# A graph-network megakernel on Trainium2: the first layer's edge work one turn further ahead, eight of its items at the turn's change

## The chip, the cores and the metric

The kernel runs on one core of a Trainium2 chip. The metric is the device time of one launch in microseconds (us); the median of three runs before the change is 2971.6 us. The engines are PE (matrix products), DVE (vector work), ACT (activations and copies), POOL (here the issuer of gathers and scatters by index, and of some loads) and SP (an issuer of DMAs alone). Each engine takes its instructions from a queue in order; semaphores tie the queues together.

## The reference

A batch of 32 graphs of 512 nodes with 256 features passes four layers, all over one adjacency matrix `adj` (about 1.6% of it and the diagonal are not zero). Layers 0 and 3 have this form:

```python
pre_u = einsum('bud,dk->buk', h, W1[:d]);  pre_v = einsum('bvd,dk->bvk', h, W1[d:])
hidden = relu(pre_u[:, :, None, :] + pre_v[:, None, :, :] + b1)
S = sigmoid(einsum('buvk,ko->buvo', hidden, W2)[..., 0] + b2[0])
a = einsum('buv,bud->bvd', S * adj, h)
m = einsum('uv,bud->bvd', adj, h) * h
z = beta1 * h + beta2 * (a @ Wa + ba) + beta3 * (m @ Wm + bm)
```

Layer 1 adds `relu((adj @ z) @ W.T + b)` to z. Layer 2 is attention with a softmax over all 512 nodes, with `adj` as its bias. `S` is needed only where `adj` is not zero: it is worked out for the edges alone.

## The kernel before

**Groups and turns.** The 32 graphs go in 8 groups of 4 (`NB`). For a group, `first` (line 806) turns each graph's features, multiplies them by W1 and writes both products of every node to a `table` in DRAM (`pre`, line 582: for each of 4 chunks of nodes matmuls L592 and L594, DVE operations L596, L599 and L600, a copy on ACT L597, and a table write on SP, L604, from one of three `puv` buffers). `edges` (line 650) works out S for the edges from the table. `middle` (line 839) does the rest of layer 0, layers 1 and 2, and, with `pre` again, the table for layer 3. A second pass of `edges` serves layer 3, and `last` (line 1094) ends it. The passes of `edges` are called edges0 and edges3 here. `middle` handles the four graphs one after another, here called batches 0 to 3. The `middle` of a group is a *turn*; 8 turns follow one another, turn 0 to turn 7, and turn 0 is short, since a part of its work is done ahead.

**An item.** A pass of `edges` has 36 items (`ITEMS`) of 128 edges. For each: `fetch` (line 682) gathers 128 table rows by index on POOL (L646) into one of five `rows` buffers, and where needed loads the other end's rows into one of three `mine` buffers (a plain 512 KB load on SP, L692, or a gather for the last four panels); DVE adds both (L731); then the relu, the product with W2 and the sum are four DVE operations (L747, even items) or one on DVE (L739) and, one item later, four sums on ACT (L717, odd items). The order of items begins with chunk 0 four times, then chunks 0 and 2 in turn. Every four items an exponential on ACT (L614) and a sigmoid on DVE (L618, L619, L675) follow some items later, and then POOL scatters the values of each item into `cells` in DRAM (`put`, L639). `own_1` does the same for the diagonal and sends it out on SP (L670). When all puts have landed, `load` (line 766) brings the cells back as SA, four loads on POOL (L772). `fetch` runs three items ahead (`LEAD`).

**The order of the work.** `sparse_path` (line 1162) gives each piece of each stream a time, in turns: `middle` of group t runs from `start` = t - 0.47 to `end` = start + 1 (turn 0 from 0 to 0.53). `weave` (line 454) sorts all pieces by time and issues them in that order, with one exception. The pieces of `first` and `last` are fillers: when their time comes they are put into a waiting list (`due`), and are taken out of it where a piece of `middle` says that PE has room (so many us, for instance 4.0 after zT, 7.0 at the first step of softmax), or when more than 12 wait, or all at once when a stream of a certain kind, such as edges0, begins:

```python
elif j == 0 and kind != "free":
    while due:
        fill()
room = run(k, j)
...
while room and room > 0.3 and due:
    room -= fill()
```

The order within an engine's queue is then settled by a scheduler at compile time that takes, of the instructions which it holds to be ready, the one that was issued first. `behind` (line 515) keeps the edge items' DVE and ACT operations from being taken forward by more than about two pieces of `middle`; fetches are not held so.

**Places.** In terms of the turn in which they run, before the change: edges3 of the group before has its items from 0.05 to 0.48 and its last puts to 0.54; `first` of the next group has its pieces from 0.18 to 0.44; edges0 of the next group has its first fetches from 0.448, its items from 0.495 to 0.94 and its last puts to 0.96; `last` of the group before runs from 0.56 to 0.16 of the turn after. A turn begins with SA's load and two matmul groups each of hWa and mhT (its product with `hT` on DVE is L801), byS (L891) and zT (L898, L896 on ACT, L899 on DVE); then come zW (L912), yT (L46, L922, L923), feats (L934), softmax (L958 to L964, and transposes L1003), the product with eT (L46, L981), `pre` for layer 3, and two transposes L992.

Of the kernel before, what the change touches and what calls it, by code (L numbers as in the profile page):

```python
# [31 lines left out]
LEAD = 3  # L32
LEAD_AT_ENDS = 5
TAIL = 6
EARLY = 20
CELLS = HALF * N
ITEMS = NC * OWN + 2 * PANELS
# [385 lines left out]
class Sparse:  # L423
# [223 lines left out]
            out=rows, out_offset=None, in_=g.table, in_offset=bass.IndirectOffsetOnAxis(ap=at, axis=0)  # L647
        )

    def edges(self, g, spare=(), own_tags=()):  # L650

# [67 lines left out]
        for n in range(lead):  # L721
            fetch(n)
            yield

        todo = [(2, lambda: self.exp_of(w, own)), (4, own_1)]
        done = 0
        for k in range(ITEMS):
            for _ in range(2 if spare and len(ready) > 2 else 1):
                put()
            rows, other = fetched.pop(k)  # L730
            self.behind(nc.vector.tensor_tensor(rows, rows, other, ALU.add))  # L731
            if k + lead < ITEMS:
                fetch(k + lead)
            if summed:
                summed.pop(0)()
# [385 lines left out]
def even(n):  # L1121
    return [1.0] * n
# [20 lines left out]
    return first + spread(even(ITEMS), a, b) + spread(even(TAIL), b, behind)  # L1143


def middle_shares(given):


    hWa = [] if given else [1.7, 1.7]
    shares = list(hWa)  # L1150
    for b in range(NB):
        more = hWa if b < NB - 1 else []
        shares += [] if given else [2.8, 2.8]
        shares += [3.4, 3.4, 1.0, 2.7]
        shares += [1.7, 3.4, 2.8, 4.5] + [0.9] * NC
        shares += [0.4, 0.4, 0.4, 1.0, 0.4, 1.0] + more + [1.5, 1.5]
        shares += [2.8, 4.5] + [0.4] * NC + [0.5, 0.5]
    return shares + [0.1]
# [3 lines left out]
def sparse_path(ctx, m, counts, xr, outr, B):  # L1162
# [10 lines left out]
    for t in range(last + 1):  # L1173
# [3 lines left out]
        if t == 0:  # L1177
            first = spread(FIRST, -0.385, -0.30)
            edges0 = edge_times(-0.292, -0.27, -0.03, -0.02, LEAD_AT_ENDS)
        elif t == 1:  # L1180
            first = spread(FIRST, -0.28, -0.06)
            edges0 = edge_times(0.02, 0.07, start - 0.06, start - 0.04)
        else:
            first = spread(FIRST, start - 0.82, start - 0.56)
            edges0 = edge_times(start - 0.552, start - 0.505, start - 0.06, start - 0.04)
        edges3 = edge_times(end + 0.003, end + 0.05, end + 0.48, end + 0.54)
        behind = end + 0.56, end + 1.16
        if t == last - 1:
            edges3 = edge_times(end + 0.003, end + 0.05, end + 0.46, end + 0.5)
            behind = end + 0.7, end + 1.06  # L1190
        if t == last:
# [2 lines left out]
            behind = end + 0.29, end + 0.45  # L1194
        streams += [
            (sp.first(g0, t * NB), first, FIRST_US),
            (sp.edges(g0, ("yT", "mhT0", "hWa0") if t == 0 else ()), edges0, ""),
            (sp.middle(g0, g3, t * NB), spread(middle_shares(t == 0), start, end), "main"),
            (
                sp.edges(g3, *((("yT", "h1", "hT1"), ("mhT0", "hWa0")) if t == last else ())),  # L1200
# [249 lines left out]
```

## Time and profile before

| what | value |
| --- | --- |
| runs of the kernel | 2968.61, 2971.6, 2972.93 us, median 2971.6 |
| profiled execution | 2998.45 us, span 2996.8 us |
| mean granted PE clock | 0.959 |
| DMA | 677.30 MB, mean 226 GB/s |
| first L891 of turns 0 to 7 | 245.2, 485.2, 824.2, 1168.8, 1514.9, 1864.3, 2207.9, 2551.5 us |

From one first L891 to the next turn 0 is 240 us long, turn 1 339, and turns 2 to 6 between 343.6 and 349.4. The page's 40 slices of the span show how evenly the engines are filled (each digit is a tenth):

```profile
## 2 busy tenths in 40 slices
PE   6367787989998999989999899989999899988998
PEld 3134344545664566546664466646565466644666
DVE  6874786889588885988778885888858896783494
ACT  3553454445344443544344443445434453453262
POOL 2662463646445673556536464466735564361183
PEclk9678998999999999999999999999999999999999
```

PE's line is near 9 from turn 1 on. DVE's line goes down every four or five slices: this is the change from one turn to the next, at which the last items of one pass of `edges` are done and the next pass still waits for its table. A busy PE is not PE at its peak, since the ends of matmuls are modelled; the starts are measured.

### The profile page before, as it was taken

Reading aid. Unit: us, or ns where it says so; the run is one execution under the profiler, and the core shown is the slowest. Engines: PE = TensorE matmul, PEld = TensorE weight load, DVE = VectorE, ACT = ScalarE, POOL = GpSimd, SP = SyncE. Lnnn points to the kernel's source line nnn. Section 1 sums busy time; section 2 is a strip of 40 time slices with the busy share of each in tenths; the row PEclk is TensorE's granted clock in tenths of the full one; section 3 lists DMA queues with packets and bytes.
Section 4 is the critical chain, followed back from the end, with each engine's and each line's share of the span. In section 5 each row is a group of like instructions: output and inputs, shape, how many; then the busy total and the mean of one; then the engine's idle time right before and its main releaser. Section 6 shows DMA issues by size and latency. Waiting matters only on the chain. (4 is left out here: it accounts for less than half of the span.)

```text
span 2996.8 us, 32453 instructions
## 1 busy us (share of the span) xinstructions
PE 2690.0 (90%) x8645; PEld 1613.9 (54%) x8646; DVE 2307.1 (77%) x6035; ACT 1336.8 (45%) x4101; POOL 1555.3 (52%) x1328
## 2 busy tenths in 40 slices
PE   6367787989998999989999899989999899988998
PEld 3134344545664566546664466646565466644666
DVE  6874786889588885988778885888858896783494
ACT  3553454445344443544344443445434453453262
POOL 2662463646445673556536464466735564361183
PEclk9678998999999999999999999999999999999999
DMA  8875657796678867787677866687677866663474
GB/s 268 286 225 169 213 174 221 233 300 203 217 217 269 268 211 227 230 262 254 209 222 247 275 207 230 216 268 253 211 228 236 303 227 197 208 211 102 148 244 150
DMA packets 302143, 677.30 MB, mean 226 GB/s; under 512 B 52608, under 2 KB 170880, under 8 KB 293760
## 3 DMA queue, kind: packets, MB, share of 16 engines
q0 software_dynamic: 122688, 414.40, 42.9%
q1 hardware_dynamic: 160304, 223.52, 23.0%
q10 hardware_dynamic: 18960, 37.24, 3.4%
q8 instruction: 70, 1.15, 0.2%
q14 instruction: 121, 0.99, 0.1%
HBM read 529.02 MB, written 146.01 MB: 225 GB/s over the span
## 5 line engine op out<-in xcount | busy, mean ns | idle before, releaser
L646 POOL DMA_INDIRECT rows<-table,iv x552 | 679.0, 1230 | 795.5 <-DMA table<-puv 262.7
L639 POOL DMA_INDIRECT cells<-s,cell x576 | 697.6, 1211 | 420.6 <-DVE s L675 243.2
L731 DVE TENSOR_TENSOR rows<-rows,mine 128x1024 f32<-128x1024 f32 x552 | 666.4, 1215 | 101.4 <-DMA rows<-table,iv 72.8
L717 ACT ACTIVATE rows<-rows 128x256 f32<-128x256 f32 x1088 | 439.6, 406 | 445.4 <-DVE rows L739 396.6
L46 PE MATMUL pst<-adj,h 128*128 128x512 f32 x1024 | 452.2, 592 | 0.0
L747 DVE SCALAR_TENSOR_TENSOR rows<-rows,L_gnn_W2bc 128x256 f32<-128x256 f32 x1120 | 414.0, 417 | 1.6
L739 DVE SCALAR_TENSOR_TENSOR rows<-rows,L_gnn_W2bc 128x1024 f32<-128x1024 f32 x272 | 329.4, 1213 | 0.4
L46 PEld LDWEIGHTS pst<-adj,h 128*128 128x128 f32 x1024 | 192.8, 190 | 219.9 <-issue 217.6
L46 PE MATMUL pst<-L_gnn_Wa,hT 128*128 128x256 f32 x1024 | 248.8, 393 | 62.9 <-DMA hT<-xT 57.8
L46 PEld LDWEIGHTS pst<-L_gnn_Wa,hT 128*128 128x128 f32 x1024 | 198.9, 199 | 103.0 <-issue 59.2
L46 PE MATMUL pst<-eT,feats 128*128 128x512 f32 x512 | 237.7, 619 | 10.9 <-ACT eT L1004 10.9
L46 PE MATMUL pst<-adjT,zW 128*128 128x512 f32 x512 | 228.2, 599 | 11.6 <-ACT zW L916 9.7
L596 DVE TENSOR_TENSOR puv<-pst,bc_L_gnn_b 128x256 f32<-128x256 f32 x256 | 104.9, 416 | 162.4 <-DMA table<-puv 89.2
L597 ACT COPY puv<-pst 128x256 f32<-128x256 f32 x256 | 93.2, 371 | 288.1 <-DVE puv L596 225.9
L1061 PE MATMUL pst<-hWa,SA 128*128 128x256 f32 x896 | 220.3, 400 | 0.0
L1061 PEld LDWEIGHTS pst<-hWa,SA 128*128 128x128 f32 x896 | 213.8, 328 | 3.7 <-issue 1.7
L717 ACT ACTIVATION_READ_ACCUMULATOR rows<-rows 128x1 f32 x1088 | 204.7, 188 | 0.0
L860 ACT COPY flat<-SA 128x512 f32<-128x512 f32 x128 | 136.7, 1128 | 136.6 <-issue 62.9
L891 PE MATMUL pst<-flat,hWa 128*128 128x512 f32 x448 | 196.8, 592 | 0.0
L592 PE MATMUL pst<-w_L_gnn_W,hT 128*128 128x512 f32 x256 | 141.5, 681 | 53.9 <-ACT hT L579 36.5
L46 PEld LDWEIGHTS pst<-eT,feats 128*128 128x128 f32 x512 | 99.9, 198 | 133.2 <-issue 113.3
L46 PEld LDWEIGHTS pst<-adjT,zW 128*128 128x128 f32 x512 | 96.5, 191 | 133.4 <-issue 114.0
(176 smaller groups left out, 3984.2 us busy)
## 6 DMA issues: line engine op xcount, KB each, us to landing
table<-puv SPq DMA_DIRECT2D x256, 256.0 KB
SA<-cells POOLq DMA_DIRECT2D x64, 1024.0 KB
h<-in_x_dram SPq DMA_DIRECT2D x64, 512.0 KB
mine<-table SPq DMA_DIRECT2D x64, 512.0 KB
hT<-xT SPq DMA_DIRECT2D x36, 512.0 KB
xT<-hT ACTq DMA_DIRECT2D x32, 512.0 KB
x2T<-yT SPq DMA_DIRECT2D x32, 512.0 KB
x2s<-x ACTq DMA_DIRECT2D x64, 256.0 KB
```

The costliest lines, as they stand in the source:

```text
L46: nc.tensor.matmul(out, lhsT, rhs, start=(n == 0), stop=(n == len(pairs) - 1))
L592: nc.tensor.matmul(pp, hT[:, 0, ks], w["W1"][:, 0::DC, :], start=True, stop=False)
L596: nc.vector.tensor_tensor(puv[:, 0, :], pp[:, 0:D], w["b1bc"], ALU.add)
L639: ins = self.nc.gpsimd.indirect_dma_start(out=g.cells[half], out_offset=bass.IndirectOffsetOnAxis(ap=at, axis=0), in_=s, in_offset=None)
L646: self.nc.gpsimd.indirect_dma_start(out=rows, out_offset=None, in_=g.table, in_offset=bass.IndirectOffsetOnAxis(ap=at, axis=0))
L717: self.behind(nc.scalar.activation(part, part, AF.Identity, accum_out=g.s[:, k, b : b + 1]))
L731: self.behind(nc.vector.tensor_tensor(rows, rows, other, ALU.add))
L739: nc.vector.scalar_tensor_tensor(by_entry, by_entry, 0.0, w2, ALU.max, ALU.mult)
L747: nc.vector.scalar_tensor_tensor(part, part, 0.0, w["W2bc"], ALU.max, ALU.mult, accum_out=at)
L860: self.nc.scalar.copy(flat[:, r, :], SA[r][:, :, b])
L891: nc.tensor.matmul(pz, hWa[:, r, cs], flat[:, r, :], start=(r == 0), stop=False)
L1061: self.nc.tensor.matmul(pz[:, k * D : (k + 1) * D], SA[r][:, cs, b], hWa[:, r, :], start=(r + k == 0), stop=(alone and k == 1 and r == NC ...
```

## The change

`first` of group t runs one turn earlier than before, at the same place within its turn (0.18 to 0.44); that of group 2 goes to turn 0, from 0.1 to 0.47. From group 2 on, edges0 is cut in two. Its first eight items (`SOON`) run one turn earlier, at the change into that turn: fetches from -0.017, items from 0 to 0.045. Then the pass stops, `mine` is forgotten and fetched anew, three fetches follow at 0.53, and the other 28 items run from 0.57 to 0.94, with the last puts to 0.96 as before. edges3 has its first fetch at 0.046 for 0.003, its items from 0.06 to 0.54 for 0.05 to 0.48, and its last puts to 0.57; `last` begins at 0.58 for 0.56. The last two groups' edges3 and `last`, and edges0 of groups 0 and 1, keep their times. Nothing that is computed changes.

```diff
+SOON = 8
...
-    def edges(self, g, spare=(), own_tags=()):
+    def edges(self, g, spare=(), own_tags=(), soon=0):
...
+        stop = soon or ITEMS
         todo = [(2, lambda: self.exp_of(w, own)), (4, own_1)]
         done = 0
         for k in range(ITEMS):
+            if k == stop:
+                stop = ITEMS
+                mine.clear()
+                for n in range(k, k + lead):
+                    fetch(n)
+                    yield
             for _ in range(2 if spare and len(ready) > 2 else 1):
                 put()
             rows, other = fetched.pop(k)
             self.behind(nc.vector.tensor_tensor(rows, rows, other, ALU.add))
-            if k + lead < ITEMS:
+            if k + lead < stop:
                 fetch(k + lead)
...
+def edge_times_soon(t0, t1, ahead, a, b, behind):
+
+    step = (t1 - t0) / SOON
+    first = [t0 - (LEAD - j) * step for j in range(LEAD)] + [t0 + j * step for j in range(SOON)]
+    step = (b - a) / (ITEMS - SOON)
+    first += [ahead + j * min(step, (a - ahead) / LEAD) for j in range(LEAD)]
+    return first + spread(even(ITEMS - SOON), a, b) + spread(even(TAIL), b, behind)
...
         else:
-            first = spread(FIRST, start - 0.82, start - 0.56)
-            edges0 = edge_times(start - 0.552, start - 0.505, start - 0.06, start - 0.04)
-        edges3 = edge_times(end + 0.003, end + 0.05, end + 0.48, end + 0.54)
-        behind = end + 0.56, end + 1.16
+            first = spread(FIRST, 0.1, 0.47) if t == 2 else spread(FIRST, start - 1.82, start - 1.56)
+            edges0 = edge_times_soon(
+                start - 1.0, start - 0.955, start - 0.47, start - 0.43, start - 0.06, start - 0.04
+            )
+        edges3 = edge_times(end + 0.046, end + 0.06, end + 0.54, end + 0.57)
+        behind = end + 0.58, end + 1.16
...
-            (sp.edges(g0, ("yT", "mhT0", "hWa0") if t == 0 else ()), edges0, ""),
+            (sp.edges(g0, ("yT", "mhT0", "hWa0") if t == 0 else (), soon=SOON if t > 1 else 0), edges0, ""),
```

## The prediction

> **What bounds the kernel now.** I read the page first. Its line of busy times says that PE is the fullest engine; the rest had to say where PE is not full.
>
> ```profile
> PE 2690.0 (90%) x8645; PEld 1613.9 (54%) x8646; DVE 2307.1 (77%) x6035; ACT 1336.8 (45%) x4101; POOL 1555.3 (52%) x1328
> ```
>
> Then I cut the trace at the first L891 matmul of every batch (the timeline of L891), and took the busy time of each engine between two such starts. The rows below are, in this order: the whole of turn 0, batches 0 to 3 of turn 3, batches 0 and 1 of turn 6, batches 0, 1 and 2 of turn 7.
>
> ```profile
> core 0: us, PE busy (x) PEld busy (x) DVE busy (x) ACT busy (x) POOL busy (x), PEclk, DMA share, GB/s
> 245.20:485.20 240.00, 195.90 (x561) 103.66 (x560) 159.06 (x423) 113.08 (x291) 94.74 (x87) 0.89 0.56 183
> 1168.80:1250.10 81.30, 81.30 (x276) 50.30 (x275) 70.67 (x176) 38.62 (x120) 37.02 (x32) 1.00 0.73 228
> 1250.10:1347.10 97.00, 81.25 (x239) 41.49 (x238) 81.33 (x247) 43.00 (x130) 57.96 (x52) 0.96 0.79 255
> 1347.10:1426.00 78.90, 76.99 (x262) 48.10 (x260) 70.13 (x176) 39.78 (x124) 47.08 (x38) 1.00 0.77 259
> 1426.00:1514.90 88.90, 88.90 (x301) 57.46 (x300) 59.81 (x168) 33.60 (x93) 46.64 (x41) 1.00 0.64 209
> 2207.90:2289.20 81.30, 81.30 (x276) 50.30 (x275) 70.61 (x176) 38.59 (x120) 37.50 (x32) 1.00 0.73 227
> 2289.20:2384.40 95.20, 81.00 (x240) 41.40 (x239) 81.24 (x246) 42.85 (x129) 59.23 (x52) 0.96 0.81 263
> 2551.50:2626.80 75.30, 74.57 (x253) 46.87 (x252) 59.16 (x148) 33.94 (x99) 30.32 (x27) 1.00 0.66 213
> 2626.80:2695.60 68.80, 57.96 (x165) 31.71 (x164) 59.50 (x150) 36.00 (x113) 47.34 (x41) 0.90 0.65 203
> 2695.60:2757.60 62.00, 53.98 (x165) 29.73 (x164) 28.41 (x94) 23.04 (x45) 10.23 (x12) 0.97 0.39 132
> ```
>
> A steady turn is bound by PE: in batches 0, 2 and 3 of turn 3 it idles 0, 1.9 and 0 us, though DVE is 87 to 89% busy in the first two. All that is left to win sits in batch 1, where `first` is woven in: 97.00 - 81.25 = 15.8 us. Turn 0, which has neither `first` nor `last` as filler, idles 44 us.
>
> Next, the waits of batch 1, of PE and of DVE (time, times, longest):
>
> ```profile
> PE pst L1003 <- DVE ex L964: 6.0, 3, 3.3
> PE pst L592 <- ACT hT L579: 3.6, 1, 3.6
> PE pst L592 <- DVE both L600: 2.1, 1, 2.1
> PE pst L934 <- DVE yT L923: 1.6, 1, 1.6
> ...
> DVE puv L596 <- DMA table<-puv: 7.1, 4, 3.4
> ```
>
> Most of batch 1's idle belongs to `first` itself: its transposes wait for a copy (L579), and its `puv` buffers hold DVE until a table write has landed (7.1 us). Edge items matter for L923 and a part of L964 alone.
>
> Last, the turn's change: DVE between the last `pre` of a turn and the first item of `edges3`, and POOL over the same stretch (brackets: idle before, releaser).
>
> ```profile
> 1159.94 0.08 DVE L600 DVE_READ_ACCUMULATOR both<-both,L_gnn_W2bc 128x1 f32 x1
> 1165.56 0.69 DVE L801 TENSOR_TENSOR mhT<-pst,hT 128x512 f32<-128x512 f32 x1 [5.54 <-PE pst L46]
> 1169.00 0.69 DVE L801 TENSOR_TENSOR mhT<-pst,hT 128x512 f32<-128x512 f32 x1 [2.74 <-PE pst L46]
> 1171.24 2.53 DVE L731 TENSOR_TENSOR rows<-rows,mine 128x1024 f32<-128x1024 f32 x2 [1.56 <-issue]
> ...
> 1142.47 1.17 POOL L772 DMA_DIRECT2D SA<-cells  x2 [1.66 <-issue]
> 1164.94 1.00 POOL L646 DMA_INDIRECT rows<-table,iv  x1 [21.30 <-DMA table<-puv]
> ```
>
> DVE has 5.5 + 2.7 + 1.6 us free here and POOL 21.3 us. The eight items are put into this hole.
>
> **The change, part by part.** The sum is made against the profiled execution: span 2996.8 us, 2998.45 us with what lies around it. The shown runs have a median of 2971.6 us, 27 us less; I carry the same difference in us over.
>
> *Turn 6 loses `first(7)`* (each `first` moves a turn ahead, so turns 0 to 5 hold the six that turns 1 to 6 held). Turn 7 already shows what batches 0 and 1 are with `last` pieces in batch 0, no `first`, and `edges3` beside them. Batch 0: 81.3 to 75.3, 6.0 less. Batch 1: 95.2 to something between 62.0 (turn 7's batch 2, hardly an edge item) and 68.8 (its batch 1, more items than here); I take 67, near the second: 28. Together -34 (bounds -32 and -39).
>
> *Turn 0 gains `first(2)`.* PE work of one `first`: four batches of 16 128x512 matmuls and 8 transposes. In the timeline four such matmuls start 1.72 us apart from the next four (1150.73, 1152.45), and 8 transposes take 0.87 (1157.60 to 1158.47): 4 x (4 x 1.72 + 0.87) = 31.0 us. What of it fills idle time follows from the weave's rule, due times against room. Softmax, where L1003 idles 31.7 us of turn 0, has room 7.0 at its first step, but the pieces come due one by one and are taken by the rooms of zT, yT and feats before it. So they fill the small waits before L912 (2.9) and L934 (2.4) of three batches in four, 4.0 us, and two 0.9 us pieces fall into softmax: 5.8 in all. 31.0 - 5.8 = 25; DVE's 16 x 3 `pre` operations (419 ns each, 20 us) stand in queues that softmax waits in, one more us: +26. Its DMAs (512 KB loads on SP, transposes out on ACT's queue, table writes on SP) come into a stretch with a DMA share of 0.56. Bounds: +19, if the pieces cover all 12.0 us that PE waits in turn 0 elsewhere than before L1003; +36, if `first` stretches a batch here as it does in batch 1 (95.2 - 67 = 28 us for 81.0 - 58.0 = 23 us of PE work).
>
> *Thinner edge items in the old places.* `edges3` goes from 36 items in 0.43 of a turn to 36 in 0.48, the rest of `edges0` from 36 in 0.445 to 28 in 0.37. Batch 1 (0.27 to 0.55 of the turn, counted from 1158.5, where a turn's first hWa matmul stands) gets 20 items for 22: 2 x 2.45 us less DVE (one item: L731 1.2 and L739 1.2, or L731 and four L747 that start 0.35 apart). Only the waits on L923, on the `s` operations and part of L964 can shrink, 2 us of 15.8; five turns (1 to 5): -10. Bounds 0 and -25 (5 a turn, all that is not `first`'s own). Batches 0, 2 and 3 have nothing to give.
>
> *The eight items at the turn's change, turns 1 to 6.* Their fetches can be issued before and between SA's loads and their table was written a turn before, so POOL's 21.3 us hide them; SA was landed by 1149.25, when ACT began to copy it, and PE wants it at 1168.80, so three fetches of 1.25 us ahead of it cost nothing (without that slack 3.8 us). On DVE all eight stand behind L600 (1160.0), since `behind` holds them there, and in the queue ahead of the middle's work: three items and the first L801, three more with own_1's sigmoid and the second L801, then two. Six items, 1160.0 + 6 x 2.45 + 2 x 0.69 + 0.57 = 1176.7; PE needs the second L801 for its third L898 matmul, 1175.66 + 0.86 = 1176.5: 0.2 us late. Behind it come two more items, a sigmoid (0.5), and two items of `edges3`, then L899: 1176.7 + 4.9 + 0.5 + 4.9 + 1.3 = 1188.3, where PE starts L912 at 1184.28 behind 5.2 us of `last` pieces: 4.0 late; or, if L899 is queued ahead of `edges3`'s first rows, 1183.4 and not late. Bounds 0 and 4.2 a turn. I take 1, nearer to nothing, as batch 2 with DVE at 89% costs PE 1.9 us in a whole batch: six turns, +6 (0 to +25).
>
> A row speaks on what such a stall adds. After the 3.60 us wait at L592 (1265.89) four matmuls took 2.51 us and two 1.91, for 1.88 and 1.02 elsewhere: 1.5 us more; after 2.08 us (1302.50) nothing. So the upper bound becomes 6 x 5.7 = +34. The Trainium skill, TensorE: Matmul & The Clock Gate, section Why this matters for your kernels, says that gaps over some 3 us put the clock back; by it a 4 us stall pays this and my 1 us does not, as the rows have it.
>
> A rule speaks against the place as such: GPSIMD Engine Reference, section Specifications, has GpSimd share its SBUF interfaces with VectorE and contend with DVE instructions of two SBUF inputs, as the items' are. The trace agrees: a fetch took 0.94 us with DVE idle (1170.03) and 1.68 beside L739 (1175.42). Eight fetches by 0.7 are 6 us of POOL's 21.3, so the sum stays by either.
>
> *Small parts.* `mine.clear()` loads chunks 0 and 2 once more: 12 x 512 KB over the run, at 226 GB/s 28 us of a DMA share of 0.74, behind work; SP's queue takes them where it took `edges0`'s own loads. The sums of item 7 are held until item 8, half a turn on, and with them one of five `rows` buffers through the whole of `edges3`. In turn 3 each fetch would then wait for the fourth release before it; 6.3 us pass from fetch to use (1164.94 to 1171.24), and at 4.1 us an item four buffers turn in 16.4 us, with 5 us of DVE and ACT in it: 5 us spare. Behind a waiting fetch on POOL stand puts, and for these only SA's load, half a turn later. own_1's diagonal goes out on SP's queue, with `edges3`'s `mine` loads behind it, which wait for the table anyway (1164.94). +2 (0 to +12).
>
> Sum: -34 + 26 - 10 + 6 + 2 = -10. Span 2986.8, median **2962 us**; by its own bounds mostly 2948 to 2969.
>
> **The rivals.**
>
> *The stall at the change decides (slower).* The eight items and `edges3`'s first two stand ahead of L801 and L899, PE waits 4.2 us and 1.5 for the clock. For it: DVE takes its queue in order. Against: 5.2 us of `last` pieces and L891's 6.9 us lie before each of the two points. Price 5.7 x 6 = 34 in place of 6: 2990. It decides from 2.7 us a turn, where the sum is zero.
>
> *Four `rows` buffers starve `edges3` (slower).* Late rows at the head of DVE's queue, 3 to 5 us a turn in place of 0.3: 2985. Against: the 5 us spare above.
>
> *The ends cancel, and the items do not leave batch 1's waits shorter (no change).* Turn 0 pays 33 for turn 6's 34, thinning gives nothing, the stall 0, small parts 2: 2973. For it: no edge item stands between 1296 and 1318 us in DVE's queue, while L964 is late.
>
> *Batch 1 was held by edge items after all (much faster).* Half of its 15.8 goes in five turns, -40: 2932. Against: the waits above.
>
> **How the numbers follow.** Forecast 0.45, stall 0.27, no change 0.15, four buffers 0.07, much faster 0.06. 0.2% is 6 us, about what this measurement can tell from none. Faster: 0.45 + 0.06 = 0.51; same 0.15; slower 0.27 + 0.07 = 0.34. The range has thinning and turn 0 at their good ends (15 + 7 us less, 2940) and the stall at 5.7 (2990), a little more on that side: 2940 to 2992.
>
> **What would show it.** Right: turn 6 some 310 us for 343.6, turn 0 some 266 for 240, batch 0 of turns 1 to 6 within 2 us of 81.3, batch 1 near 94. Wrong: an idle PE before L898 or L912 in batch 0 of each turn (the stall); L731 waiting for `rows` in `edges3` (buffers); batch 1 at 97 (no thinning); turn 0 at 275 or more.

## The result, and the profile after

The changed kernel has a median of 3023.87 us (four runs, 3014.21 to 3028.1) beside 2970.67 us for the kernel before in the same set of runs: ratio 1.0167, interval 1.0149 to 1.0186. It is 1.7% slower, and the time lies above the predicted range.

The profiled execution of after has a span of 3021.0 us and took 3022.74, as its other runs did. The profiled execution of before took 27 us more than its other runs, so the two traces explain a difference of 24.2 us in the span and not the whole 53 us of the medians; what the remainder is no trace shows. The second profiles of both kernels (e0 and e5 below) differ by 36.2 us. The engines' busy times are as they were. The work is the same; it waits elsewhere.

```profile
PE 2686.0 (89%) x8645; PEld 1623.0 (54%) x8646; DVE 2313.8 (77%) x6035; ACT 1335.8 (44%) x4101; POOL 1559.0 (52%) x1328
```

Line numbers of after are those of before plus 1 up to `sums` (L592 is L593, L646 is L647, L717 is L718) and plus 8 from the items' additions on (L731 is L739, L739 is L747, L747 is L755, L772 is L780, L891 is L899, L923 is L931, L934 is L942). Cut at the first L899 of every batch, these are turn 0, batches 0 to 3 of turn 3, and batches 0, 1 and 2 of turn 6; the columns are start and end, length, and the busy time of each engine.

```profile
core 0: us, PE busy (x) PEld busy (x) DVE busy (x) ACT busy (x) POOL busy (x), PEclk, DMA share, GB/s
241.40:505.50 264.10, 223.73 (x657) 120.46 (x656) 182.25 (x499) 120.47 (x318) 95.32 (x90) 0.92 0.63 206
1202.60:1286.60 84.00, 81.74 (x275) 50.19 (x274) 77.90 (x197) 41.45 (x130) 42.91 (x33) 1.00 0.77 235
1286.60:1369.10 82.50, 76.81 (x240) 40.45 (x239) 72.45 (x216) 41.42 (x125) 50.55 (x43) 1.00 0.80 256
1369.10:1456.60 87.50, 76.61 (x253) 47.76 (x252) 68.76 (x183) 38.61 (x120) 50.13 (x43) 0.94 0.74 255
1456.60:1547.90 91.30, 90.57 (x309) 59.03 (x308) 62.97 (x174) 33.57 (x90) 49.06 (x43) 1.00 0.64 220
2247.90:2325.70 77.80, 75.27 (x253) 46.58 (x252) 69.76 (x174) 36.77 (x115) 40.74 (x32) 1.00 0.77 228
2325.70:2401.20 75.50, 58.35 (x165) 32.44 (x164) 65.86 (x177) 36.83 (x116) 52.69 (x47) 0.89 0.66 212
2401.20:2485.20 84.00, 76.65 (x254) 47.49 (x253) 67.82 (x180) 38.85 (x120) 47.58 (x41) 0.98 0.76 250
```

Against before: batch 1 of turn 3 fell from 97.0 to 82.5 us, but batch 0 rose from 81.3 to 84.0, batch 2 from 78.9 to 87.5, batch 3 from 88.9 to 91.3. In batch 2 PE is busy 76.6 of 87.5 us. Its waits and DVE's and POOL's there (engine, line, what for: total, times, longest), one view each:

```profile
PE pst L942 <- DVE yT L931: 9.6, 1, 9.6
```

```profile
DVE rows L739 <- DMA rows<-table,iv: 15.4, 3, 8.7
```

```profile
POOL rows L647 <- ACT rows L718: 9.5, 3, 7.2
POOL SA L780 <- DMA cells<-s,cell: 7.1, 2, 4.8
```

The chain is read in POOL's queue over the same stretch (start, length, instruction; in brackets the idle time before it and what ended it), and then in DVE's:

```profile
1377.77 0.58 POOL L780 DMA_DIRECT2D SA<-cells  x1 [4.79 <-DMA cells<-s,cell]
1378.65 1.02 POOL L647 DMA_INDIRECT rows<-table,iv  x1 [0.30 <-issue]
1379.97 1.74 POOL L640 DMA_INDIRECT cells<-s,cell  x1 [0.30 <-DVE hT L907]
...
1385.03 1.98 POOL L640 DMA_INDIRECT cells<-s,cell  x1 [0.30 <-issue]
1387.31 0.99 POOL L647 DMA_INDIRECT rows<-table,iv  x1 [0.30 <-issue]
1388.31 0.60 POOL L780 DMA_DIRECT2D SA<-cells  x1
1391.27 1.08 POOL L780 DMA_DIRECT2D SA<-cells  x2 [2.36 <-DMA cells<-s,cell]
1392.65 1.00 POOL L647 DMA_INDIRECT rows<-table,iv  x1 [0.30 <-issue]
```

```profile
1384.94 1.23 DVE L739 TENSOR_TENSOR rows<-rows,mine 128x1024 f32<-128x1024 f32 x1 [2.35 <-DMA rows<-table,iv]
1394.83 1.22 DVE L739 TENSOR_TENSOR rows<-rows,mine 128x1024 f32<-128x1024 f32 x1 [8.66 <-DMA rows<-table,iv]
...
1403.58 1.23 DVE L739 TENSOR_TENSOR rows<-rows,mine 128x1024 f32<-128x1024 f32 x1 [4.43 <-DMA rows<-table,iv]
...
1405.54 0.69 DVE L931 TENSOR_TENSOR yT<-yT,hT 128x512 f32<-128x512 f32 x1
```

`last`'s first load of SA waits 4.79 us at the head of POOL's queue, for cells that `edges3`'s puts have only just written. Behind it stand one fetch, four puts of `edges3`'s other half (e3 below shows whose they are), and then the fetch of a further row that `edges0` needs at its restart. That fetch goes out at 1387.31, and DVE's addition of its row waits 8.66 us. The fetch after it goes out at 1392.65, behind the other three loads of SA, and DVE waits another 4.43 us for its row. L931 stands in DVE's queue behind both additions, and PE waits 9.6 us for L931's yT.

### The profile page after: what moved, and what is told of

Same layout as the page of the kernel before. It is cut to its first block, busy times and chain, and to the rows that moved or that the text cites. A ratio compares the mean times of both kernels' runs of the same rounds, so it can differ in the third digit from the quotient of the medians.

```text
span 3021.0 us, 32437 instructions
## 1 busy us (share of the span) xinstructions
PE 2686.0 (89%) x8645; PEld 1623.0 (54%) x8646; DVE 2313.8 (77%) x6035; ACT 1335.8 (44%) x4101; POOL 1559.0 (52%) x1328
## 5 line engine op out<-in xcount | busy, mean ns | idle before, releaser
L647 POOL DMA_INDIRECT rows<-table,iv x552 | 678.2, 1229 | 898.4 <-ACT rows L718 246.7
L739 DVE TENSOR_TENSOR rows<-rows,mine 128x1024 f32<-128x1024 f32 x552 | 666.7, 1218 | 187.5 <-DMA rows<-table,iv 165.8
L718 ACT ACTIVATE rows<-rows 128x256 f32<-128x256 f32 x1088 | 439.7, 407 | 541.1 <-DVE rows L747 539.6
L755 DVE SCALAR_TENSOR_TENSOR rows<-rows,L_gnn_W2bc 128x256 f32<-128x256 f32 x1120 | 414.6, 418 | 1.4
L747 DVE SCALAR_TENSOR_TENSOR rows<-rows,L_gnn_W2bc 128x1024 f32<-128x1024 f32 x272 | 331.2, 1219 | 0.6
L47 PE MATMUL pst<-eT,feats 128*128 128x512 f32 x512 | 231.1, 605 | 28.0 <-ACT eT L1012 28.0
L718 ACT ACTIVATION_READ_ACCUMULATOR rows<-rows 128x1 f32 x1088 | 205.7, 189 | 0.0
L868 ACT COPY flat<-SA 128x512 f32<-128x512 f32 x128 | 137.8, 1137 | 153.4 <-PE pst L47 84.9
L942 PE MATMUL pst<-WT,yT 128*128 128x257 f32 x512 | 134.8, 419 | 71.9 <-DVE yT L931 71.9
L899 PE MATMUL pst<-flat,hWa 128*128 128x512 f32 x448 | 196.8, 592 | 0.0
```

Of the source, the lines that this page charges most:

```text
L47: nc.tensor.matmul(out, lhsT, rhs, start=(n == 0), stop=(n == len(pairs) - 1))
L647: self.nc.gpsimd.indirect_dma_start(out=rows, out_offset=None, in_=g.table, in_offset=bass.IndirectOffsetOnAxis(ap=at, axis=0))
L718: self.behind(nc.scalar.activation(part, part, AF.Identity, accum_out=g.s[:, k, b : b + 1]))
L747: nc.vector.scalar_tensor_tensor(by_entry, by_entry, 0.0, w2, ALU.max, ALU.mult)
L755: nc.vector.scalar_tensor_tensor(part, part, 0.0, w["W2bc"], ALU.max, ALU.mult, accum_out=at)
L868: self.nc.scalar.copy(flat[:, r, :], SA[r][:, :, b])
```

## The experiments

The kernel before had medians between 2971 and 2997 us in the sets of runs, so kernels are compared by their ratio to the before of their own set. The traces are cut as above: turns 0, 1 and 6 whole, and the mean of turns 2 to 5 for batches 0 to 3, in us.

| kernel | ratio (95%) | turn 0 | turn 1 | batches 0, 1, 2, 3 | turn 6 |
| --- | --- | --- | --- | --- | --- |
| before, first profile | 1 | 240.0 | 339.1 | 81.3, 95.0, 80.0, 89.5 | 343.6 |
| before, second (e0) | 1 | 239.3 | 340.3 | 81.3, 93.4, 81.0, 90.0 | 343.4 |
| after, first | 1.0167 (1.0149 to 1.0186) | 264.2 | 349.4 | 84.4, 85.4, 87.2, 91.3 | 326.8 |
| after, second (e5) | 1.0143 (1.0127 to 1.0160) | 262.2 | 354.8 | 85.0, 85.3, 87.4, 91.3 | 331.6 |
| e1 first alone | 1.0047 (1.0021 to 1.0073) | 261.8 | 337.7 | 81.3, 93.9, 82.0, 89.7 | 329.9 |
| e2 sums at once | 1.0014 (0.9994 to 1.0033) | 261.7 | 341.1 | 83.0, 85.4, 85.5, 91.3 | 326.2 |
| e3 puts at the change | 1.0082 (1.0055 to 1.0108) | 263.8 | 351.3 | 84.5, 85.8, 84.7, 91.5 | 325.1 |
| e6 e2, last later | 1.0359 (1.0338 to 1.0380) | 264.2 | 357.0 | 87.8, 87.2, 85.8, 99.9 | 326.5 |
| e8 e2, fetches sooner | 1.0065 (1.0046 to 1.0085) | 264.3 | 345.3 | 83.5, 84.8, 84.6, 91.3 | 322.7 |
| e9 e2, load behind fetches | 0.9998 (0.9976 to 1.0019) | 263.1 | 341.3 | 83.3, 84.9, 82.9, 91.3 | 323.3 |
| e11 e2, group 2 whole | 1.0018 (0.9997 to 1.0039) | 254.9 | 346.3 | 84.5, 85.2, 83.7, 92.0 | 323.6 |
| e14 e2, edges3 sooner | 0.9992 (0.9974 to 1.0011) | 263.0 | 343.9 | 85.7, 87.6, 77.5, 91.3 | 319.1 |
| e16 e14, sums held | 1.0212 (1.0193 to 1.0232) | 263.2 | 349.5 | 87.9, 95.5, 76.5, 91.3 | 324.7 |
| e17 e14, four items | 0.9978 (0.9958 to 0.9998) | 260.3 | 328.8 | 83.3, 89.0, 76.9, 90.6 | 323.1 |
| e10 before, mine on POOL | 1.0043 (1.0017 to 1.0069) | 233.6 | 344.0 | 81.3, 95.8, 79.0, 92.0 | 348.3 |
| e15 before, edges0 later | 1.0068 (1.0043 to 1.0092) | 239.1 | 338.5 | 81.3, 93.5, 77.7, 93.5 | 345.5 |
| e18 before, copy on DVE | 1.0122 (1.0088 to 1.0155) | 239.2 | 340.2 | 82.5, 97.4, 81.1, 90.0 | 352.8 |
| e20 before, e14's places | 1.0037 (1.0019 to 1.0056) | 239.2 | 333.0 | 82.1, 89.8, 82.0, 94.6 | 345.5 |

**The kernel before once more (e0), and first alone (e1).** e1 is the kernel before with the one line

```diff
-            first = spread(FIRST, start - 0.82, start - 0.56)
+            first = spread(FIRST, 0.1, 0.47) if t == 2 else spread(FIRST, start - 1.82, start - 1.56)
```

> The kernel before, unchanged, for a second profiled execution: the first (span 2996.8 us) took 27 us more than the median of the plain runs. If profiled executions as such run longer, this one has a span near 2997 too and turns 1 to 6 of 339 to 349 us again. If the first was an odd one, the span is near 2970, and some 27 us are missing from the turns: the turns' lengths of after have then to be read against these shorter ones, and turn 6 of after lost less than it seems, or the steady turns got longer than they seem.

> Half of the change alone: first one turn further ahead, edges0 and edges3 as before. Theory (the split of edges0 costs the time: late rows hold DVE and yT in batch 2 and in batch 0 of turns 1 to 6): batch 2 of a steady turn is back at 78 to 80 us, batch 1 stays near 95, turn 0 is near 264, turn 6 near 310, and the time is 2960 to 2972, the kernel before or a little less. Rival (first one turn ahead costs it, by its table writes and loads in another place): batch 2 stays at 86 to 88 and the time is above 3000.

e0's span is 2999.4 us and its turns 2 to 5 are as long as the first's (345.7 and 345.8 us in the mean), so before's first trace was no odd one. Whether profiled executions run longer as such stays open: e0's 3001.12 us lie within the other runs of its set (2981.26 to 3005.71 us, median 2991.22). e1 took 0.5% more than before, between the totals of the two theories (before's time or less; some 1% more). Batch 2 was near the theory's (82.0, with 80.0 and 81.0 in the two traces of before), so it is the split that makes batch 2 long. Batch 1 stayed at 93.9: `first` of another group does not shorten it. But the ends do not cancel. Turn 0 pays 22.5 us and turn 6 gets back 13.5. Turn 0, and batches 0 and 1 of turn 6 of e1:

```profile
244.20:506.00 261.80, 223.57 (x657) 119.71 (x656) 176.86 (x487) 120.57 (x314) 91.99 (x86) 0.91 0.61 196
2231.00:2308.30 77.30, 74.79 (x254) 46.76 (x252) 67.60 (x165) 37.41 (x116) 39.72 (x33) 1.00 0.70 218
2308.30:2393.10 84.80, 58.11 (x165) 31.93 (x164) 66.80 (x192) 35.34 (x109) 58.08 (x50) 0.84 0.72 233
```

Without `first`, PE has 58.1 us to do in batch 1, but DVE still has the edge items, and PE idles 26.7 of the 84.8 us, 20.1 of them for DVE.

**Item 7's sums at once (e2), the puts at the change (e3), after again (e5).** e2 and e3 are the changed kernel with one of these edits:

```diff
-                if spare:
+                if spare or k + 1 == stop:
                     summed.pop(0)()
```

```diff
                 todo.pop(0)[1]()
+            if k + 1 == stop:
+                while ready:
+                    put()
             yield
```

> The changed kernel, but the four sums of item 7 are issued at once, so that no rows buffer is held from the turn's change to the restart of edges0. Theory one (POOL's queue at the restart: a load of SA for last waits there for the cells, and four puts stand before the late fetches): batch 2 keeps its 86 to 88 us, and batch 0 too, time within 8 us of 3023. Theory two (one of five rows buffers held starves edges3 and the restart): the waits of POOL for rows fall from 247 and 241 us to near the 103 and 106 of before, batch 0 goes back to 81, batch 2 gains as well, time 2990 or less.

> The changed kernel, but the four puts of items 0 to 3 are issued at the turn's change, not one each at the restart. Theory one in its one form (the puts, some 1.7 us of POOL each, delay the fetch of item 11): the waits of L739 for rows at the restart (8.7 us) fall by about 6 us, the wait of PE for yT in batch 2 (10 to 12 us a turn) by half or more, time 2985 to 3000. In its other form (the load of SA that waits 4.8 us for the cells at the head of POOL's queue): batch 2 gains 2 us or less a turn, time 3010 to 3023. Theory two (a held rows buffer): no change, 3020 or more.

> The changed kernel itself, run again beside its variants, since the runs of before on another chip had a median 20 us above the first ones. If the cost of the change does not hang on the chip, the ratio is again near 1.017; then issuing the sums of item 7 at once (1.0014) was worth 1.5%, and issuing the four puts at the turn's change (1.0082) 0.8%. If it is near 1.008, the first measurement was an unlucky pair and the puts were worth nothing.

After held its ratio (1.0143). One line for the held sums takes nine tenths of the loss away (1.0014 for 1.0143), most of it in turn 1 (13.7 us against e5) and batches 0 and 2 (2 us each in turns 2 to 5). The two ratios come from different sets; in e5's own set the kernel nearest to e2 is e8 below, at 1.0065, so the line is worth 0.8 to 1.3%. Theory two's time for it came nearly (2997.4 us for 2990 or less), its sign did not: the waits of POOL for rows, 247 and 241 us in after, are 261 and 231 in e2. What did change is the time from a row's fetch to its use, worked out from the starts of L647 and L739, in turns 2 to 5:

```
                 batch 0: median   batch 1: median, below 8 us
before           14.0 us           13.1 us          12 of 75
after             9.2 us            9.1 us          29 of 71
e2                10.5 us           12.0 us          10 of 72
```

With four buffers rows come late more often: in batch 1, 29 rows had less than 8 us, and 10 in e2. In batch 0 most of the fall from 14.0 us is still there in e2, so that part is not the held buffer's. DVE's waits for rows fell from 172.0 us (64 times) in e5 to 147.3 (44) in e2; before has 72.8 and 81.2. e3's puts brought less (1.0082). Its trace shows why it could not do what was expected of it: four puts still stand between SA's load and the next fetch in batch 2 of turn 3, though those of items 0 to 3 had gone out at the change. They are `edges3`'s.

**Which of load and fetch comes first (e6, e7, e8, e9).** All contain e2. e6: `last` from 0.66 of a turn in place of 0.58. e7: e6 with e3's edit. e8: the restart's fetches from 0.49 in place of 0.53. e9: the load gets an order behind the last fetch issued before it:

```diff
+        self.fetched = ins.ins.name
...
+            if layer == 3:
+                order = mybir.DependencyInfo(mybir.DependencyClass.NoSync, mybir.DependencyReason.DATA)
+                self.tc.add_manual_dep(ins.ins, self.fetched, order, reason="behind the fetches before")
```

> Item 7's sums at once, and last begins 0.08 of a turn later, so that its loads of SA no longer stand in POOL's queue ahead of the restart's fetches. Theory one (the load that waits for cells at the head of POOL's queue makes the rows late): the wait of 6 to 9 us of DVE for rows at the restart goes, batch 2 falls from 85 to 86 us to 80 or less, time 15 to 30 us under the version with the sums at once alone, ratio 0.991 to 0.997. Rival (the four puts between are what delays, or the items themselves): batch 2 gains 2 us or less, ratio 1.000 to 1.002.

> As the version with item 7's sums at once and last later, and with the four puts of items 0 to 3 issued at the turn's change too. If the puts at the restart matter beside the load, batch 2 gains 2 to 5 us more than without, ratio 0.988 to 0.995; if they do not, it is within 0.2% of the version without; if they take POOL's time where SA's loads for the turn itself stand, batch 0 gets longer by 1 to 2 us and the ratio is higher.

> Item 7's sums at once, and the restart's three fetches 0.04 of a turn earlier, ahead of edges3's last puts and of the load of SA instead of behind them; last at its place. Theory one: the rows of items 8 to 10 are there in time, but the fetch of item 11 still stands behind the waiting load and the puts, so batch 2 gains about half of what the later load gives, ratio 0.995 to 1.000. Rival (five rows buffers do not suffice for both passes): POOL waits there for a buffer, SA's load and edges3's last puts get later, batch 2 stays at 85 us, ratio 1.000 or more.

> Item 7's sums at once, and the loads of SA for last may not be queued on POOL ahead of a row fetch that was issued before them; everything else in its place. (In the version with last 0.08 later the load stood in POOL's queue where it was before, behind the same fetch, so that run didn't move it; it moved last's matmuls out of batch 2.) The load now stands two fetches later. Theory one (the load at the head of POOL's queue makes the rows late): DVE's wait for rows at the restart falls from 9 us to 4 or less, batch 2 from 85 to 86 us to 80 to 82, ratio 0.990 to 0.998. Rival (edges3's end itself, so late that no order helps): batch 2 within 2 us, ratio 1.000 to 1.005.

e6 was a miss that teaches: 3.6% slower than before. The scheduler took the load forward to the very place where it had been, and only `last`'s matmuls moved. Batches 2 and 3 of turn 4 of e6:

```profile
1755.80:1844.90 89.10, 72.39 (x214) 42.26 (x213) 68.71 (x184) 37.10 (x111) 46.67 (x42) 0.90 0.72 232
1844.90:1945.00 100.10, 98.16 (x341) 65.86 (x340) 63.45 (x173) 33.54 (x91) 49.18 (x43) 1.00 0.64 211
```

Batch 2 has 214 matmuls in place of 253 and is no shorter; the 31 that batch 3 got beyond its 310 make it 9 us longer. Here a filler that missed the idle time it was to fill cost its full length. e7 was no better (ratio 1.0387). e8 left batch 2 within 1 us of e2's, as the rival had it. In e9 two fetches of batch 2 stand ahead of the first load where e2 has one, and batch 2 gained 2.6 us, with a ratio of 0.9998. That lies between the theory's (80 to 82 us) and the rival's: the order counts for a part. All four loads still stand ahead of the next fetch, and the puts are as late as in e2.

**edges3 sooner (e14), with the sums held (e16), with four items (e17).** e14 is e2 with the places below; e16 is e14 without e2's edit; e17 is e14 with `SOON = 4`.

```diff
-                start - 1.0, start - 0.955, start - 0.47, start - 0.43, start - 0.06, start - 0.04
+                start - 1.0, start - 0.955, start - 0.51, start - 0.47, start - 0.06, start - 0.04
-        edges3 = edge_times(end + 0.046, end + 0.06, end + 0.54, end + 0.57)
+        edges3 = edge_times(end + 0.046, end + 0.06, end + 0.5, end + 0.53)
```

> Item 7's sums at once, edges3's items end at 0.50 and its puts at 0.53 of a turn (in place of 0.54 and 0.57) and edges0 starts again at 0.49 and 0.53 (in place of 0.53 and 0.57), so that the cells have landed when the load of SA comes, with a fetch between load and load as before the change. Theory one: batch 2 falls from 85 to 86 us to 79 to 81 as before the change, batch 1 stays near 85, ratio 0.985 to 0.993. Rival (the thinner edges3 was what made batch 1 short): batch 1 goes to 90 or more and takes back what batch 2 gains, ratio 0.999 to 1.004.

> As the version with edges3 and the restart sooner, but with item 7's sums held until the restart as in the changed kernel. It prices the held rows buffer where nothing waits for cells. Theory (four buffers in place of five shorten the time from fetch to use in edges3 from 12 to 20 us to 6 to 10 and DVE's queue then stands before late rows): batches 0 and 2 1.5 to 3 us longer a turn, turn 1 10 us, ratio 1.006 to 1.013. Rival (it only hurt together with the waiting load): ratio 0.998 to 1.002.

> As the version with edges3 and the restart sooner (item 7's sums at once), but with four items at the turn's change in place of eight, the other 32 from 0.53 to 0.94. If the eight items' DVE work is what makes batch 0 longer (81.3 to 85.7 us, and 73.5 to 86.6 in turn 1), both fall by about half of that, 2 us a turn and 6 in turn 1; batch 1 or 2 gets some of it back; ratio 0.994 to 0.999. If what stands at the change costs it whatever the number (the loads of mine, own_1's diagonal), batch 0 stays within 1 us of 85.7 and the ratio at 0.999 to 1.002.

In e14 batch 2 came back to 77.5 us, and the waits of SA's loads for cells fell from 64.8 us (16 times) in e2 to 21.9 (7 times). So its length came with these places. e14 moves `edges3`'s end and the restart at once; e8 had moved the restart's fetches alone and gained 1 us, so the late end of `edges3` is the likely part, which no run moved alone. The theory's ratio did not come; the rival's did (0.9992), but not by its way alone: batch 1 rose to 87.6 and batch 0 to 85.7. e16 prices the held buffer where few loads wait for cells (22.8 us, 7 times). The waits of DVE for rows in e14:

```profile
DVE rows L739 <- DMA rows<-table,iv: 55.6, 36, 6.9
```

and in e16:

```profile
DVE rows L739 <- DMA rows<-table,iv: 106.9, 60, 12.5
```

Twice the waits, and turns 2 to 5 are 351.2 us for 342.1: here one buffer of five is 9 us a turn, and 2.2% in the ratio (between two sets). The median time from fetch to use falls from 11.3 to 9.1 us in batch 0 and from 11.9 to 9.9 in batch 1. Batch 1 takes most of it (87.6 to 95.5 us), where the expectation had batches 0 and 2. With the change's own places the same buffer cost 3.8 us a turn and 13.7 in turn 1 (e5 against e2): what it costs hangs on the places. e17 is the price of the eight items themselves. Batches 0 of turns 1 and 4 of e17:

```profile
501.20:574.30 73.10, 61.91 (x187) 34.25 (x186) 65.80 (x169) 37.82 (x118) 40.96 (x32) 0.91 0.76 233
1508.00:1591.30 83.30, 83.30 (x284) 51.85 (x283) 70.81 (x177) 38.90 (x120) 39.54 (x32) 1.00 0.71 234
```

With four items PE does not idle in batch 0 (83.30 of 83.30 us, with 284 matmuls for the 276 of before), and turn 1's batch is as before (73.1). With eight it was 85.7 and 86.6. So a good half of what batch 0 lost was the number of items. e17 is 0.2% faster than the kernel before, and the only version here whose interval lies below 1, if barely.

**What a first costs where PE idles (e11).** e2, but group 2 is not split, has before's places, and its `first` runs from 0.15 to 0.78, into turn 1's first batch, which has no filler (turn 1's `edges3` and `last` have before's places too):

```diff
+            first = spread(FIRST, 0.15, 0.78) if t == 2 else spread(FIRST, start - 1.82, start - 1.56)
```

> Item 7's sums at once, and group 2's edges are not split and stand where they stood before the change, so its first has time to 0.78 (from 0.15) and reaches into the first batch of turn 1, where PE has no filler and idles 15 us. If the price of the ends is what their places make it: turn 0 falls from 262 to some 250, turn 1 stays at 335 to 341, time 6 to 15 us under the version with the sums at once alone, ratio 0.996 to 0.999. Rival (a first costs its 23 us wherever it goes, since pieces fill no idle time there either): the sum of turns 0 and 1 stays at 603 us, ratio 1.000 to 1.003.

The rival's: turn 0 gave 6.8 us back and turn 1 paid 5.2, turns 0 and 1 are 601.2 us for 602.8 and were 579 before. The turns pay some 22 us in either place, though PE idles 44 us in turn 0 of before.

**Why batch 1 became shorter (e10, e15, e18, e19, e20).** All but e19 are edits of the kernel before. e10: the `mine` loads issued by POOL. e15: `edges0` later. e18: first's copy on DVE. e19: that in e17. e20: e15 with `edges3` in e14's place.

```diff
-                    nc.sync.dma_start(t, places[c, 0])
+                    nc.gpsimd.dma_start(t, places[c, 0])
```

```diff
-            nc.scalar.copy(hT[:, c, :], pt)
+            nc.vector.tensor_copy(hT[:, c, :], pt)
```

```diff
-            edges0 = edge_times(start - 0.552, start - 0.505, start - 0.06, start - 0.04)
-        edges3 = edge_times(end + 0.003, end + 0.05, end + 0.48, end + 0.54)
+            edges0 = edge_times(start - 0.51, start - 0.47, start - 0.06, start - 0.04)
+        edges3 = edge_times(end + 0.046, end + 0.06, end + 0.5, end + 0.53)
```

> The kernel before, with the plain loads of mine issued by POOL instead of SP. It tests why the change made batch 1 some 10 us shorter although DVE has as many items there: in the trace of before a mine load waits 5.5 us at the head of SP's queue in batch 1, with first's table writes behind it, for which DVE then waits (8.7 us at L596). Theory (SP's queue): batch 1 falls from 94 to 86 to 90 us, DVE's wait for table writes there to 5 us or less, ratio 0.985 to 0.993. Rival (batch 1 gained by other means, such as the order of DVE's queue): batch 1 stays at 92 to 95, ratio 0.999 to 1.004, above 1 if POOL's fetches then wait behind the loads.

> The kernel before, with the whole of edges0 0.035 to 0.04 of a turn later (fetches from 0.49, items from 0.53 to 0.94 in place of 0.448 and 0.495), nothing else. It tests what made batch 1 some 8 to 10 us shorter after the change. Theory (two or three items that leave the end of batch 1, where two passes of edges overlap): batch 1 falls from 94 to 86 to 89 us without any split and without a first moved, batch 2 rises by 1 to 3, ratio 0.988 to 0.996. Rival (it is the eight items that run elsewhere, or the first that belongs to a later group): batch 1 stays at 92 or more, ratio 0.998 to 1.004.

> The kernel before, with first's copy of its turned features (two 128x512 copies a graph) on DVE in place of ACT. In batch 1 of before that copy stands in ACT's queue behind four sums of an odd edge item, which wait 3.0 to 3.1 us each for the item's DVE operation, and PE waits 3.6 us for the copy. Theory (batch 1's length is set by where the odd items' sums stand relative to that copy, and the split only shifted them): PE's idle before first's first matmuls falls from 7 to 9 us to 2 to 4, batch 1 from 93.4 to 87 to 90 without any split, ratio 0.991 to 0.996. Rival (DVE is as far behind as ACT, since ACT only waits for DVE): the wait stays, batch 1 at 92 to 96, ratio 0.999 to 1.004.

> The version with four items at the turn's change and edges3 sooner, with first's copy on DVE too. Theory (ACT's queue): its batch 1 falls from 89 to 85 to 87 and the rest stays, ratio 0.990 to 0.995. Rival (the split already took what the copy's place can give, and DVE is fuller): ratio 0.997 to 1.002.

> The kernel before, with edges3 from 0.06 to 0.50 (puts to 0.53) in place of 0.05 to 0.48 (0.54), and the whole of edges0 later as in the run that did that alone (batch 1 stayed at 93.5): the places of the version with edges3 and the restart sooner, but no item split off and no first moved. Theory (batch 1 is set by the place of edges3's items against first's copy, in the queues of DVE and ACT): batch 1 falls from 93.5 to 87 to 90 with batch 0 at 81.3 and batch 2 at 78, ratio 0.988 to 0.996. Rival (the split itself shortens batch 1, since edges3 then meets another queue, or the first that belongs to another group does): batch 1 stays at 92 or more, ratio 1.000 to 1.008.

The place of the `mine` loads in SP's queue is not it: batch 1 of e10 stayed at 95.8. DVE's wait for table writes stayed as well (6.7 us a batch in turns 2 to 5, 7.1 in e0), so e10 says nothing on that wait. Nor is it the number of items alone: e15 has 16 or 17 in batch 1 where before has 18 or 19, and stayed at 93.5. ACT's queue in batch 1 of turn 4 of e0 then showed where `first` waits, with PE's row beside it:

```profile
1606.06 0.42 ACT L717 ACTIVATE rows<-rows 128x256 f32<-128x256 f32 x1 [3.08 <-DVE rows L739]
1606.47 0.40 ACT L717 ACTIVATE rows<-rows 128x256 f32<-128x256 f32 x1
1606.88 0.40 ACT L717 ACTIVATE rows<-rows 128x256 f32<-128x256 f32 x1
1607.28 1.05 ACT L579 COPY hT<-pst 128x512 f32<-128x512 f32 x2
```

```profile
1607.89 3.78 PE L592 MATMUL pst<-w_L_gnn_W,hT 128*128 128x512 f32 x4 [3.60 <-ACT hT L579]
```

The transposes end at 1604.3. Their copy stands behind the sums of an odd item, which wait for that item's product on DVE. On DVE itself PE waits longer for the copy. Waits of PE in batch 1 of turn 4 of e18:

```profile
PE pst L592 <- DVE hT L579: 6.9, 1, 6.9
```

So e18's rival held, and more: 1.2% slower, and e19 took e17 from 0.9978 to 1.0119 (1.0079 to 1.0158). e20 changes nothing but the places and shows that the wait moves with them: PE's idle time before first's matmuls L592 and L594, from the trace's gaps in the batches 1 of turns 2 to 5, is 0.9 to 1.9 us where e15 has 4.4 to 7.3, and batch 1 falls to 89.8 with no split and no `first` moved. Batch 1 of turn 4 of e15, and of e20:

```profile
1590.00:1683.20 93.20, 80.33 (x239) 41.56 (x238) 74.69 (x232) 41.12 (x121) 58.83 (x51) 0.96 0.79 263
```

```profile
1597.00:1685.00 88.00, 78.95 (x239) 41.63 (x238) 76.34 (x234) 42.81 (x127) 53.62 (x46) 0.98 0.80 262
```

The kernel as a whole did not gain by it (1.0037, the rival's range): batch 2 rose by 4.3 us against e15.

But this is not what shortened batch 1 in after. PE's idle time in batch 1, from the same gaps, a mean over turns 2 to 5, in us (waits above 0.15 us; `busy` is the length without them, for 238 matmuls each):

```
          length  idle   for first's hT   for ex and yT (L1003, pre for layer 3)   busy
before     95.1   14.0        5.7                     6.4                          81.1
e15        93.5   12.2        5.5                     6.0                          81.2
e20        89.7   10.5        1.6                     6.3                          79.3
after      85.4    7.4        4.2                     1.9                          78.0
e2         85.4    7.6        2.8                     2.4                          77.8
```

In after the wait for `first`'s copy is still 4.2 us, in two pieces below 3 us each. What went are the waits for the softmax's ex and for yT, 6.4 to 1.9 us, and 3.1 us of busy time. Busy time goes with the granted clock of batch 1, 0.960 in before and 0.985 in after: before has five waits of over 3 us in these four batches, after has none. The waits for ex and yT are 1.4 to 2.4 us in all nine traces in which `edges0` takes up its items again at 0.57 and `edges3` ends at 0.54, and 3.0 to 6.4 in the others, in which the items of `edges0` begin at 0.53 or sooner. No run moved these places without the split, so the cause of the shorter batch 1 stays open.

## Why the prediction was wrong, by its steps

Its terms, against the first two traces (the head, turn 7 and the tail together make -3 us):

| step | predicted | measured |
| --- | --- | --- |
| turn 0 gains first(2) | +26 | +24.2 |
| turn 6 loses first(7) | -34 | -16.8 |
| thinner items, batch 1 | -2 a turn | -9.7 a turn (turns 2 to 5), -4.9 (turn 1) |
| eight items, batch 0 | +1 a turn | +3.1 a turn (turns 2 to 5), +10.3 (turn 1) |
| batches 2 and 3 | nothing | +9.0 a turn (turns 2 to 5), +4.9 (turn 1) |
| small parts | +2 in all | the held buffer alone, e5 against e2: +3.8 a turn (turns 2 to 5), +13.7 (turn 1), +5.4 (turn 6) |

The last row is no further part of the difference: it is spread over the batches of the other rows.

**The step that failed is "Small parts".** It saw that item 7's sums hold one of five `rows` buffers through `edges3`, and put this at next to nothing, with "5 us spare", a mean over one round of four buffers. Measured, the buffer cost some 34 us over turns 1 to 6, and 0.8 to 1.3% of the time (e2 and e8 against e5); at e14's places it cost 9 us a turn (e16). What counts is not the mean: with four buffers rows come late more often, and a late row stands at the head of DVE's queue. With item 7's sums at once the time is 2975 to 2990 us by the first set's before, inside the range though not the gain that was forecast. The rival "four `rows` buffers starve edges3" was the right one, and its sign came: L739 waited for rows 165.8 us in after, L731 72.8 in before (though the sign does not tell it from the late load of SA: e2 has 147.3). It got 0.07. Its price of 3 to 5 us a turn is what turns 2 to 5 show; that turn 1 pays 13.7 it did not have.

**What the sum did not have at all** is SA's load for `last`. The text put "puts, and for these only SA's load, half a turn later" behind a waiting fetch, and did not turn it round: the change also moves `edges3`'s last puts to 0.57, a hundredth of a turn from the load and beside the restart's fetches. The load waits for its cells, and the fetches wait behind it. With e14's places batch 2 is 8.0 us a turn shorter than in e2. The text gave batches 2 and 3 "nothing to give", and did not ask what they could lose.

**Turn 0** was right in size, in part by luck: PE's work there grew by 27.8 us (195.90 to 223.73) and not by 31.0, and 3.7 us of it filled idle time and not 5.8. e11 adds that the one other place tried is no cheaper. **Turn 6** had the right sign and half the size. Batch 1 was taken from turn 7's batches 1 and 2, in which DVE has fewer edge items; here it is 75.5, not 67, and batch 2 pays the waits of every other turn (84.0 for 77.3).

**The thinner items** gave five times what was taken for them. That fewer items in batch 1 do it is not shown (e15 has fewer and stayed). The step was right that a part of the idle time is `first`'s own wait for a copy, but not that edge items matter "for L923 and a part of L964 alone": the copy itself stands behind an edge item's sums. How far an item's place moves that wait (e20) could have been read in ACT's queue. What went in after were mostly the waits on L964 and yT, more of them than the 2 us that the text allowed, and the busy time that a lower clock had cost, which the sum did not have. (That no edge item stands in DVE's queue from 1296 to 1318 us of before holds from 1298 on.)

**The eight items at the turn's change** cost PE nothing in turns 2 to 6 where the prediction looked, before L898 and L912 (L906 and L920 now); in turn 1 PE waits 2.2 us before L906. In batch 0 of turn 3 PE's waits, as the profile puts them down, are these two:

```profile
PE pst L942 <- DVE yT L931: 1.5, 1, 1.5
PE pst L47 <- ACT eT L1012: 0.7, 1, 0.7
```

So the rival of the stall had the wrong place, and its price of 5.7 us a turn stands against 3.1, of which 2.0 go with the held buffer (85.0 us in e5, 83.0 in e2). Turn 1's 10.3 us were not in the sum: there batch 0 has no filler, lasts only 73 us, and the eight items' twenty microseconds of DVE work (8 x 2.45) did not hide in it, where four items' did (e17).

## What to carry to other kernels

One buffer of a rotating set that is held across a phase costs what it does to the lead of every later load, not the mean spare time; a step that is split must let go of everything at the cut. When a load waits for scattered writes in an in-order queue, look at what is issued behind it, and end the writes early enough; moving the load's time in the program did not move it in the queue here (e6). Before an engine's idle time is put down to one stage, read the queue of the engine that releases it: the copy that matters may stand behind another stage's wait. And before a shorter stage is put down to the wait that an experiment moved, see whether that wait is gone from the trace in question.

## What the runs showed of the hardware

A long wait of PE costs more than its length:

```profile
1406.37 5.59 PE L942 MATMUL pst<-WT,yT 128*128 128x257 f32 x16 [9.63 <-DVE yT L931]
```

After the 9.63 us wait in turn 3 of after the sixteen 128x257 matmuls of L942 took 5.59 us; sixteen of the same line took 3.63 us in turn 4 of e14 (at 1733.78), behind other matmuls without a wait. The granted clock was 1.00 when PE fell idle at 1396.7, 0.50 from 1400 to 1410, and 1.00 again from 1411. The Trainium skill, TensorE: Matmul & The Clock Gate, section Why this matters for your kernels, has the clock fall back after gaps of some 3 us; these rows agree with it, and the 2.0 us are what it cost here.

The Trainium skill, Perfetto Trace Analysis, section Tensor Engine Instruction (MATMUL, LD_WEIGHTS), says in passing that ACT, DVE and GpSimd take their instructions strictly in order. Both chains found here rest on that, and the rows agree: the fetch issued at 1387.31 behind SA's load, and the copy at 1607.28 behind the sums.

Between the seven sets of runs, on different chips as far as the record names them, the median of one unchanged kernel lay between 2970.67 and 2996.98 us, a spread of 0.9%, while the interval of a ratio within one set is 0.3 to 0.8% wide. Differences of this change's size can only be read inside a set.
